# A two-layer graph attention kernel: column maxima by halves, and the second layer's first chunk prepared inside the first layer

## The chip, the cores and the metric

The kernel runs on one core of a Trainium2 chip. The metric is the device time of one execution in microseconds (us); shorter is better. The engines are called PE (TensorE, matrix products), DVE (VectorE), ACT (ScalarE), POOL (GpSimd) and SP (SyncE, which here only issues DMA transfers). [...]

## What is computed

```python
def gat_layer(x, W, adj):                  # twice, W of 512 x 1024
    Wh, Ws = split(x @ W, 2, axis=-1)
    a = softmax(Wh @ Ws.T, axis=-1) * adj   # 3327 x 3327
    return leaky_relu(a @ Wh + x, 0.01)
h = layernorm(x + gat_layer(gat_layer(x, W0, adj), W1, adj))
ba, bw = maximum(sign(h), 0), sign(weight)
return layernorm(h + relu(adj @ (ba @ bw.T)))
```

x is 3327 x 512, adj is 3327 x 3327 with about one per cent of ones, everything in float32.

## The kernel before, in words

The 3327 rows make 26 tiles of 128 (P), 13 pairs of tiles (NQ), and 7 chunks of 512 columns (NC); a half is 256 columns (HW), the output rows of one pair. A float32 product of two-by-two blocks is done with seven instead of eight block products (Strassen and Winograd's form, `seven`, L168). Its operands need sums of blocks (`left_sums` L203, `right_sums` L210), and its seven products share three PSUM banks, called X, Y and Z, which copies (L145, L183, L196 or L597, L632) and adds (L186, or L607, L622, L628) empty.

`project` (L297) makes, for one layer, the values x @ Wh-part and, with the product of the two weight halves (`product_m`, L281, named m and msum), the queries for the scores. It works from x transposed, one chunk at a time. Later chunks are loaded in a form whose 32 x 32 blocks are already in place (`load_laid`) and are turned by DVE (L338). The first chunk is loaded in rows and turned by 16 PE transposes (L326 in layer 1, L332 in layer 2) with copies out of PSUM (L333). `keys` (L371) makes the key sums and stores the blocks for the scores (`xs_d`) from POOL's queue. The queries are stored as `gs_d` and loaded again by chunk as `gs` (a tile with two buffers, shared with the weight sums `wsum`).

`attention` (L549) computes the transposed scores and then the values. Its loop (L985 to L1024) goes over v from -34 to 168. In step v it does the block products of the values for `steps[v]`, where step 13 g + q is half g and key pair q, and the scores for `ahead[v + 30]`, so the scores run 30 steps ahead; near the end of a layer only values are left. A step takes about 6 us while both are in it, and 3 us or somewhat more with one of them. In each step the work is a list of pairs (position, function); it is sorted by position, and that order is the order of the instructions on each engine. So a position sets only an order, not a time. The work of a step is:

- from the scores: the bank's adds and copies, then the running maximum over key pairs (`maximum`, L639 to L650). The first key pair of a half copies (L648), the others take a maximum (L650);
- `shift` of the pair three steps ahead at 0.0 (DVE, L736, subtracts the column maximum) and its exponential at 0.12 (ACT, L739);
- for the pair two steps ahead, `running` at 0.01 (the sum for the softmax; DVE, a copy L745 for q = 0 and an add L747 otherwise) and `masked` at 0.4 (DVE, L752, times adj), followed by block sums on POOL (L790 to L793);
- in some steps the same sums for adj in 8 bits (`halved_sums` at 0.6, `halved` at 0.61, `exact` at 0.62; L755 to L781);
- `values` (PE, L817), and at the last key pair `take_out` (L827 to L851), with which DVE empties the accumulators. It is called at positions (i + 1.4) / 7 for i = 1, 3, 5, 6, that is 0.343, 0.629, 0.914 and 1.057;
- one function of `finish` (L853 to L934) at 0.7: the reciprocal sum (`norm`: POOL's sum of totals L856, PE's pz L865), the residuals (L881, L884), and in the last layer sign, PE transposes (L905) and the binary linear product;
- entries of a dictionary `early`. In layer 1 these are the loads, turns (L253, L260) and products (L289) of layer 2's weights in the last 15 to 30 steps.

`column_max` (L666 to L709) comes when a chunk's scores are complete. It puts three functions for both halves of the chunk into the next step: the fold of two row blocks (-0.04), the maximum across partitions (0.36: turns, reductions, and small copies between groups of 32 partitions, L697 among them), and the turn back into the tile `off` (0.9, L704). The first `shift` of the chunk stands in the step after the next.

`finale` (L1114) first makes layernorm constants (`constants`: the root on ACT L1125, then DVE L1126, L1127), then the sums for the last tile pair's binary product (`product_sums`, L1192, whose instructions show as L211 to L214), and then aggregates adj @ xw (PE, L1109).

Of the kernel before, what the change touches and what calls it, by code (L numbers as in the profile page):

```python
# [9 lines left out]
F32 = mybir.dt.float32  # L10
# [20 lines left out]
def kernel(  # L31
# [193 lines left out]
    ch_lane, acc_lane, tr_lane = (ps_ch, "ch"), (ps_acc, "acc"), (ps_tr, "tr")  # L225
    w_rows, w_laid, wT, m_of, wsum_of = {}, {}, {}, {}, {}

# [6 lines left out]
    def transpose_w(l, h, k, lane):  # L234
        pool, tag = lane
        pt = pool.tile([P, D], F32, tag=tag, name=f"pwT_{l}_{h}_{k}")
        for d in range(KD):
            nc.tensor.transpose(pt[:, ts(d, P)], w_rows[l, h, d][:, ts(k, P)], ident)
        wT[l, h, k] = slot([P, D], F32, f"wTs_{l}_{h}_{k}")
        copy_out(1 if h == 0 else k, wT[l, h, k], pt)  # L240

# [55 lines left out]
    def project(l, pre):  # L297
# [18 lines left out]
        def transpose_first(lane):  # L316

            pool, tag = lane
            xTs[0] = pre.tile([P, KD, CW], F32, tag="xT", bufs=2, name=f"xT_{l}_0")
            pts = [pool.tile([P, CW], F32, tag=tag, name=f"pxt_{l}_{k}") for k in range(KD)]  # L320
            xts = [t.rearrange("r (p k) -> r k p", k=KD) for t in rows_of[0]]
            if l == 0:

                for a in range(CT):
                    for k in range(KD):
                        nc.tensor.transpose(pts[k][:, ts(a, P)], xts[a][:, k], ident)  # L326
                for k in range(KD):
                    copy_out(k, xTs[0][:, k], pts[k])
                return
            for k in range(KD):  # L330
                for a in range(CT):
                    nc.tensor.transpose(pts[k][:, ts(a, P)], xts[a][:, k], ident)  # L332
                nc.scalar.copy(xTs[0][:, k], pts[k])  # L333

        def transpose_x(c, a):
            if a == 0:
                xTs[c] = pre.tile([P, KD, CW], F32, tag="xT", bufs=2, name=f"xT_{l}_{c}")
            nc.vector.transpose(  # L338
                xTs[c][:, :, ts(a, P)].rearrange("p k (r v) -> p r k v", v=B),
                rows_of[c][a].rearrange("p r (u k) -> p r k u", u=B),  # L340
            )


        load_x(0)
        wa = pre.tile([P, KD, D], F32, tag="wa", bufs=1, name=f"wa_{l}")
# [6 lines left out]
        load_x(1)  # L352
        transpose_first(acc_lane)
        parts = sums_w(l) if l == 0 else []
# [16 lines left out]
        def keys(c, a, between=lambda: None):  # L371

            q = c * CT // 2 + a
            xT = xTs[c]
            j1, j2 = ts(2 * a, P), ts(2 * a + 1, P)
            s12 = slot([P, 2, 2, P], F32, f"s12_{l}_{q}")
            s34 = slot([P, 2, 2, P], F32, f"s34_{l}_{q}")
            of = {
                A11: xT[:, 0:2, j1], A12: xT[:, 2:4, j1], A21: xT[:, 0:2, j2],
                A22: xT[:, 2:4, j2], S1: s12[:, 0], S2: s12[:, 1], S3: s34[:, 0],  # L380
                S4: s34[:, 1],
            }
            left_sums(
                *(of[i] for i in (A11, A12, A21, A22, S1, S2, S3, S4)), between=between
            )
            to = xs_d[l][q]
            for raw in (A11, A12, A21, A22):
                nc.gpsimd.dma_start(out=to[:, raw], in_=of[raw])
            nc.gpsimd.dma_start(out=to[:, S1 : S2 + 1], in_=s12)
            nc.gpsimd.dma_start(out=to[:, S3 : S4 + 1], in_=s34)  # L390
            return of
# [157 lines left out]
    def attention(l, att):  # L549
# [5 lines left out]
        sc, top, total, off, adj, acc, gs, xs, ch = ({} for _ in range(9))  # L555
        asum, ws, out_ = {}, {}, {}
        WS = 3
# [27 lines left out]
        def scores(c, q, s):  # L585
# [53 lines left out]
            def maximum(i):  # L639
                t = sc[i, q]  # L640
                if q == NQ - 1 and pad:
                    nc.vector.tensor_scalar(
                        t[:, 1], t[:, 1], there[:, 0:1], there[:, 1:2], ALU.mult, ALU.add
                    )
                if q == 0:
                    top[i] = att.tile([P, 2, HW], F32, tag=f"top{i % 2}", bufs=1,
                                      name=f"top_{l}_{i}")
                    nc.vector.tensor_copy(top[i], t)  # L648
                else:
                    nc.vector.tensor_tensor(top[i], top[i], t, ALU.max)  # L650

            if s == 1:

                after.append((-0.05, lambda: maximum(mine[0])))
                if q == NQ - 1:
                    after.extend(column_max(c))
            if len(mine) == 1:
# [7 lines left out]

        def column_max(c):  # L666

            mine = halves_of(c)
            n = len(mine) * HW // B


            part = small.tile([P, CW // B], F32, tag="mxq", bufs=1, name=f"mxq_{l}_{c}")
            quad = small.tile([P, P // B, CW // B], F32, tag="mx4", bufs=1,
                              name=f"mx4_{l}_{c}")
            whole = small.tile([P, CW // B], F32, tag="mx", bufs=1, name=f"mx_{l}_{c}")

            def fold():
                for g in mine:
                    nc.vector.tensor_tensor(
                        top[g][:, 0], top[g][:, 0], top[g][:, 1], ALU.max  # L680
                    )

            def across():
                w = HW // B
                for i, g in enumerate(mine):
                    nc.vector.transpose(top[g][:, 1], top[g][:, 0])
                    nc.vector.reduce_max(
                        part[:, ts(i, w)],
                        top[g][:, 1].rearrange("p (r u) -> p r u", u=B), axis=AX.X,
                    )  # L690
                for a in range(P // B):
                    nc.vector.tensor_copy(quad[:B, a, :n], part[ts(a, B), :n])
                nc.vector.reduce_max(
                    whole[:B, :n], quad[:B, :, :n].rearrange("p a r -> p r a"), axis=AX.X
                )
                for a in range(1, P // B):
                    nc.vector.tensor_copy(whole[ts(a, B), :n], whole[:B, :n])  # L697

            def back():
                w = HW // B  # L700
                for i, g in enumerate(mine):
                    off[g] = att.tile([P, 1, HW], F32, tag=f"off{i}", bufs=1,
                                      name=f"off_{l}_{g}")
                    nc.vector.transpose(  # L704
                        off[g][:, 0].rearrange("p (r u) -> p r u", u=B),
                        whole[:, ts(i, w)].unsqueeze(2).to_broadcast([P, w, B]),
                    )

            return [(-0.04, fold), (0.36, across), (0.9, back)]  # L709

# [26 lines left out]

        def exponential(g, q):
            nc.scalar.activation(sc[g, q], sc[g, q], AF.Exp)  # L739

        def running(g, q):

            if q == 0:
                total[g] = att.tile([P, 2, HW], F32, tag="total", name=f"total_{l}_{g}")
                nc.vector.tensor_copy(total[g], sc[g, q])  # L745
            else:
                nc.vector.tensor_tensor(total[g], total[g], sc[g, q], ALU.add)  # L747
# [53 lines left out]
        def values(g, q):  # L801
# [21 lines left out]
            if q == NQ - 1:  # L823
                got += [((i + 1.4) / 7, lambda i=i: take_out(g, i)) for i in (1, 3, 5, 6)]
            return got
# [27 lines left out]
        def finish(g):  # L853
# [72 lines left out]
            if not last:  # L926
# [3 lines left out]
            return [  # L930
                norm, lambda: residual(0), lambda: (sign(0), fetch(1)), *free,
                lambda: turn(0), lambda: linear(0), lambda: residual(1), lambda: sign(1), *free,
# [3 lines left out]
        if last:  # L936

            early, wts = {}, {}

# [7 lines left out]
        else:  # L947

            end = len(ahead) - LOOK
            early, parts = {}, []  # L950
            for i in range(2 * KD):
# [11 lines left out]
            early[end + 3] = [(0.9, lambda: load_w(l + 1, 0))]  # L963
            n = len(steps) - end - 2
            early[end + 2] = [(0.2, begin_m)]
            for i, do in enumerate(product_m(l + 1, ch_lane)):
                early.setdefault(end + 2 + i * n // (KD * KD), []).append(
                    (0.3 + 0.4 * (i % 2), do)
                )
            early.setdefault(end + 7, []).append((0.6, lambda: parts.extend(sums_w(l + 1))))  # L970
            for i in range(4):
                early.setdefault(end + 7 + i, []).append((0.65, lambda: parts.pop(0)()))
# [141 lines left out]
    def finale(att):  # L1114
# [69 lines left out]
        def check():  # L1184
# [4 lines left out]
            nc.vector.tensor_copy(flag_i, flag)  # L1189

        constants()
        product_sums(NQ - 1)  # L1192
        load_h(0)
# [142 lines left out]
```

## Time and profile before

| what | value |
|---|---|
| time, median of 3 runs | 2627.36 us (2627.24 to 2629.74) |
| the profiled execution's own time | 2626.88 us |
| its span, first to last instruction | 2625.1 us (1.78 us lie outside) |
| granted PE clock, mean | 0.998 of full speed |
| DMA | 639 MB, 243 GB/s over the span |
| ACT L739, exponential of 128x512 | x338, 631 ns each |
| DVE L650, maximum of 128x512 | x312, 726 ns each |
| DVE L736 / L747 / L752 | x338 / x312 / x338, 735 / 745 / 705 ns each |

The profile is one execution. A row of the timeline gives start and duration in us, the engine, the line, the operation, output <- inputs, the shape and a count; brackets hold the idle time before it and the instruction whose end released it ("issue" where the profile names none). PEld is the loading of weights, which overlaps the matmuls. An engine's row of waits gives what it waited for, the total, how often, and the longest. POOL's durations are rough. The line numbers are those of the kernel before.

### The profile page before, as it was taken

How to read it: one execution, taken by the hardware profiler on the slowest of the kernel's cores; microseconds unless marked ns; L12 is line 12 of the kernel's file. 1: busy time of each engine (PE TensorE's matmuls, PEld its weight loads, DVE VectorE, ACT ScalarE, POOL GpSimd, SP SyncE). 2: the span in 40 equal slices, each digit the busy share in tenths (PEclk: the TensorE clock that was granted, in tenths of full speed). 3: DMA queues.
4: the chain of work that ended last, by engine and by line, in shares of the span. 5: the costliest groups of instructions: out<-in, count | busy, mean ns of one | idle time of the engine just before them, and what ended most of it. 6: DMA issues, size and time to landing. Idle time of an engine off the chain costs nothing. (4 is left out here: it accounts for less than half of the span.)

```text
span 2625.1 us, 40169 instructions
## 1 busy us (share of the span) xinstructions
PE 2582.4 (98%) x12552; PEld 2238.6 (85%) x12552; DVE 2116.0 (81%) x4376; ACT 785.9 (30%) x1954; POOL 1104.1 (42%) x2025
## 2 busy tenths in 40 slices
PE   9999999999999999999999999999999999999998
PEld 6888888888888888887888888888888888888787
DVE  6764888899898896777875689989899898767876
ACT  2323332333333332211332333333333333222143
POOL 3640344444444444546562144444444444455510
PEclk9999999999999999999999999999999999999999
DMA  6855777787777776787875668777787776688775
GB/s 209 296 193 180 240 242 269 232 276 249 263 245 246 267 241 223 236 254 245 284 243 179 226 223 283 250 242 265 238 283 245 236 271 233 226 263 264 260 249 171
DMA packets 308055, 639.16 MB, mean 243 GB/s; under 512 B 34855, under 2 KB 175745, under 8 KB 306298
## 3 DMA queue, kind: packets, MB, share of 16 engines
q1 hardware_dynamic: 272140, 530.29, 61.7%
q0 software_dynamic: 35664, 106.18, 11.0%
q8 instruction: 103, 1.69, 0.3%
q14 instruction: 118, 0.97, 0.1%
q10 hardware_dynamic: 30, 0.03, 0.0%
HBM read 529.69 MB, written 106.67 MB: 242 GB/s over the span
## 5 line engine op out<-in xcount | busy, mean ns | idle before, releaser
L580 PE MATMUL pZ<-gs,xs 128*128 128x256 f32 x2496 | 636.8, 379 | 2.0 <-ACT u L597 1.7
L790 POOL TENSOR_TENSOR as<-s 128x128 f32<-128x128 f32 x338 | 163.8, 485 | 1042.9 <-DVE s L752 888.2
L580 PEld LDWEIGHTS pZ<-gs,xs 128*128 128x128 f32 x2496 | 473.2, 190 | 69.2 <-ACT u L597 3.6
L817 PE MATMUL acc<-ws,s 128*128 128x256 f32 x1352 | 402.2, 379 | 0.0
L817 PE MATMUL acc<-wh,s 128*128 128x256 f32 x1352 | 355.7, 379 | 0.6 <-DVE s L752 0.4
L817 PE MATMUL acc<-ws,as 128*128 128x256 f32 x1352 | 348.0, 380 | 7.0 <-issue 4.0
L739 ACT ACTIVATE s<-s 128x512 f32<-128x512 f32 x338 | 213.4, 631 | 428.4 <-DVE s L736 428.3
L580 PE MATMUL pY<-gs,xs 128*128 128x256 f32 x1248 | 320.6, 379 | 1.7 <-ACT p L597 1.7
L817 PEld LDWEIGHTS acc<-ws,as 128*128 128x128 f32 x1352 | 255.9, 190 | 48.8 <-issue 8.9
L817 PEld LDWEIGHTS acc<-wh,s 128*128 128x128 f32 x1352 | 256.7, 190 | 36.2 <-DVE s L752 1.4
L817 PEld LDWEIGHTS acc<-ws,s 128*128 128x128 f32 x1352 | 256.0, 190 | 34.5
L650 DVE TENSOR_TENSOR top<-top,s 128x512 f32<-128x512 f32 x312 | 222.5, 726 | 73.1 <-ACT s L637 53.3
L580 PEld LDWEIGHTS pY<-gs,xs 128*128 128x128 f32 x1248 | 236.8, 190 | 35.0 <-ACT p L597 2.8
L736 DVE TENSOR_TENSOR s<-s,off 128x512 f32<-128x512 f32 x338 | 248.4, 735 | 0.1
L752 DVE TENSOR_TENSOR s<-s,adj 128x512 f32<-128x512 f32 x338 | 238.3, 705 | 8.9
L747 DVE TENSOR_TENSOR total<-total,s 128x512 f32<-128x512 f32 x312 | 232.5, 745 | 0.0
L792 POOL TENSOR_TENSOR as<-s 128x128 f32<-128x128 f32 x338 | 208.6, 617 | 26.5
L597 ACT COPY u<-pZ 128x256 f32<-128x256 f32 x312 | 115.7, 371 | 323.2 <-PE pZ L580 322.6
L817 PE MATMUL acc<-wh,as 128*128 128x256 f32 x676 | 202.5, 381 | 0.0
L791 POOL TENSOR_TENSOR s<-s 128x128 f32<-128x128 f32 x338 | 186.7, 552 | 27.4
L793 POOL TENSOR_TENSOR as<-s,as 128x128 f32<-128x128 f32 x338 | 181.8, 538 | 26.5
L622 DVE TENSOR_TENSOR s<-p,u 128x256 f32<-128x256 f32 x156 | 67.6, 433 | 139.0 <-ACT u L597 137.9
(218 smaller groups left out, 3864.0 us busy)
## 6 DMA issues: line engine op xcount, KB each, us to landing
ws<-ws_d SPq DMA_DIRECT2D x338, 512.0 KB, 3.8
xs<-xs_d SPq DMA_DIRECT2D x182, 512.0 KB, 5.9
adj<-in_adjT_dram SPq DMA_DIRECT2D x324, 256.0 KB, 4.3
xs<-xs_d SPq DMA_DIRECT2D x156, 384.0 KB, 6.4
gs_d<-gsp POOLq DMA_DIRECT2D x88, 256.0 KB, 3.0
gs<-gs_d SPq DMA_DIRECT2D x12, 1792.0 KB, 11.5
adj_d<-ab POOLq DMA_DIRECT2D x169, 112.0 KB, 3.9
ahl<-adj_d SPq DMA_DIRECT2D x78, 224.0 KB, 4.9
```

Source lines behind the costliest of these rows:

```text
L580: nc.tensor.matmul(ch[bank], xs[c, q, a][:, k], gs[c][:, b, k], start=(start and k == 0), stop=(k == 1), skip_group_check=True,)
L597: nc.scalar.copy(ch[name], ch[bank])
L650: nc.vector.tensor_tensor(top[i], top[i], t, ALU.max)
L736: nc.vector.tensor_tensor(s, s, off[g].to_broadcast([P, 2, HW]), ALU.subtract)
L739: nc.scalar.activation(sc[g, q], sc[g, q], AF.Exp)
L747: nc.vector.tensor_tensor(total[g], total[g], sc[g, q], ALU.add)
L752: nc.vector.tensor_tensor(s, s, adj[g, q], ALU.mult)
L790: nc.gpsimd.tensor_tensor(s3, a11, a21, ALU.subtract)
L791: nc.gpsimd.tensor_tensor(a21, a21, a22, ALU.add)
L792: nc.gpsimd.tensor_tensor(s2, a21, a11, ALU.subtract)
L793: nc.gpsimd.tensor_tensor(s4, a12, s2, ALU.subtract)
L817: nc.tensor.matmul(acc[g][i // 2][:, i % 2], a[i], b[i], start=(q == 0 and i % 2 == 0), stop=(q == NQ - 1), skip_group_check=True,)
```

## The change

1. The column maximum is made half by half. For the even half of a chunk all four pieces (fold, turn, across, back) stay in the step after the last score; the odd half's fold and turn go a step later, its `across` another, its `back` another.
2. At the first key pair nothing is copied: `top` comes from a maximum of the first two pairs' scores, and `total` from a second exponential of the first pair.
3. `take_out` stands at 0.34, 0.59, 0.91 and 1.06.
4. Layer 2's first chunk of x is loaded in laid form (16 transfers on SP, steps 160 to 163 of layer 1's attention), turned by DVE in steps 165 and 166, and its key sums are made in step 167. Its tile takes a buffer of `gs`. `project` of layer 2 then neither loads nor turns it.
5. `product_m` begins one step later, spread over 14 instead of 15 steps.
6. In the last layer the finish of half 11 (`g == NQ - 2`) gets an empty slot before `norm`, so all of it comes a step later.
7. `finale` calls `product_sums` before `constants`.
8. `transpose_w` copies with ACT only (layer 1's weights at the start; two of the eight copies were on DVE).

```diff
+    def turn_x(xT, a, xt):
+        nc.vector.transpose(
+            xT[:, :, ts(a, P)].rearrange("p k (r v) -> p r k v", v=B),
+            xt.rearrange("p r (u k) -> p r k u", u=B),
+        )
+    def key_sums(l, q, a, xT, between=lambda: None):
...
+        left_sums(
+            *(of[i] for i in (A11, A12, A21, A22, S1, S2, S3, S4)), between=between
+        )
+        return of
...
-        copy_out(1 if h == 0 else k, wT[l, h, k], pt)
+        nc.scalar.copy(wT[l, h, k], pt)
...
-        load_x(0)
+        if l == 0:
+            load_x(0)
+        else:
+            xTs[0] = x_first[l]
...
-        transpose_first(acc_lane)
+        if l == 0:
+            transpose_first(acc_lane)
...
-                if q == 0:
+                if q == 1:
...
-                    nc.vector.tensor_copy(top[i], t)
-                else:
+                    nc.vector.tensor_tensor(top[i], sc[i, 0], t, ALU.max)
+                elif q > 1:
                     nc.vector.tensor_tensor(top[i], top[i], t, ALU.max)
...
-                    after.extend(column_max(c))
+                    after.extend(column_max(mine[0]))
+                    for i in mine[1:]:
+                        for n, (_, do) in zip((2, 2, 3, 4), column_max(i)):
+                            early.setdefault(v + n, []).append((0.68, do))
...
-            return [(-0.04, fold), (0.36, across), (0.9, back)]
+            return [(-0.04, fold), (0.2, turn), (0.5, across), (0.7, back)]
...
         def exponential(g, q):
-            nc.scalar.activation(sc[g, q], sc[g, q], AF.Exp)
-
-        def running(g, q):
-
             if q == 0:
                 total[g] = att.tile([P, 2, HW], F32, tag="total", name=f"total_{l}_{g}")
-                nc.vector.tensor_copy(total[g], sc[g, q])
-            else:
+                nc.scalar.activation(total[g], sc[g, q], AF.Exp)
+            nc.scalar.activation(sc[g, q], sc[g, q], AF.Exp)
+
+        def running(g, q):
+
+            if q > 0:
                 nc.vector.tensor_tensor(total[g], total[g], sc[g, q], ALU.add)
...
-                got += [((i + 1.4) / 7, lambda i=i: take_out(g, i)) for i in (1, 3, 5, 6)]
+                got += [
+                    (at, lambda i=i: take_out(g, i))
+                    for i, at in ((1, 0.34), (3, 0.59), (5, 0.91), (6, 1.06))
+                ]
...
-                norm, lambda: residual(0), lambda: (sign(0), fetch(1)), *free,
+                *(free if g == NQ - 2 else []), norm, lambda: residual(0), lambda: (sign(0), fetch(1)), *free,
...
-            n = len(steps) - end - 2
+            n = len(steps) - end - 3
...
-                early.setdefault(end + 2 + i * n // (KD * KD), []).append(
+                early.setdefault(end + 3 + i * n // (KD * KD), []).append(
...
+            laid, n = [], len(steps)
+            for a in range(CT):
+                early.setdefault(n - 9 + a, []).append((0.9, lambda a=a: load_first(a)))
+                early.setdefault(n - 4 + a // 2, []).append((0.45, lambda a=a: turn_first(a)))
+            for a in range(CT // 2):
+                early.setdefault(n - 2, []).append((0.6 + a / 10, lambda a=a: keys_of_first(a)))
...
+        product_sums(NQ - 1)
         constants()
-        product_sums(NQ - 1)
```

`load_first(a)` calls `load_laid` on SP for 128 rows of the first layer's output, `turn_first(a)` calls `turn_x`, and `keys_of_first(a)` calls `key_sums`.

More of the change, by code (lines that the diff above doesn't have):

```diff
@@ L225 @@
     ch_lane, acc_lane, tr_lane = (ps_ch, "ch"), (ps_acc, "acc"), (ps_tr, "tr")
-    w_rows, w_laid, wT, m_of, wsum_of = {}, {}, {}, {}, {}
+    w_rows, w_laid, wT, m_of, wsum_of, x_first, keys_first = ({} for _ in range(7))
+    def turn_x(xT, a, xt):
[4 more added lines that the diff above has]
+    def key_sums(l, q, a, xT, between=lambda: None):
+        j1, j2 = ts(2 * a, P), ts(2 * a + 1, P)
+        s12 = slot([P, 2, 2, P], F32, f"s12_{l}_{q}")
+        s34 = slot([P, 2, 2, P], F32, f"s34_{l}_{q}")
+        of = {
+            A11: xT[:, 0:2, j1], A12: xT[:, 2:4, j1], A21: xT[:, 0:2, j2],
+            A22: xT[:, 2:4, j2], S1: s12[:, 0], S2: s12[:, 1], S3: s34[:, 0],
+            S4: s34[:, 1], "s12": s12, "s34": s34,
+        }
+        left_sums(
+            *(of[i] for i in (A11, A12, A21, A22, S1, S2, S3, S4)), between=between
+        )
+        return of
     def load_w(l, h):
@@ L321, in transpose_first @@
             xts = [t.rearrange("r (p k) -> r k p", k=KD) for t in rows_of[0]]
[L322 to L326, printed above, removed]
+            for a in range(CT):
                 for k in range(KD):
-                    copy_out(k, xTs[0][:, k], pts[k])
-                return
+                    nc.tensor.transpose(pts[k][:, ts(a, P)], xts[a][:, k], ident)
             for k in range(KD):
-                for a in range(CT):
-                    nc.tensor.transpose(pts[k][:, ts(a, P)], xts[a][:, k], ident)
-                nc.scalar.copy(xTs[0][:, k], pts[k])
+                copy_out(k, xTs[0][:, k], pts[k])
         def transpose_x(c, a):
@@ L337, in transpose_x @@
                 xTs[c] = pre.tile([P, KD, CW], F32, tag="xT", bufs=2, name=f"xT_{l}_{c}")
[L338 to L341, printed above, removed]
-        load_x(0)
+            turn_x(xTs[c], a, rows_of[c][a])
+        if l == 0:
+            load_x(0)
+        else:
+            xTs[0] = x_first[l]
         wa = pre.tile([P, KD, D], F32, tag="wa", bufs=1, name=f"wa_{l}")
@@ L373, in keys @@
             q = c * CT // 2 + a
[L374 to L385, printed above, removed]
+            of = keys_first.pop((l, q), None) or key_sums(l, q, a, xTs[c], between)
             to = xs_d[l][q]
@@ L388, in keys @@
                 nc.gpsimd.dma_start(out=to[:, raw], in_=of[raw])
-            nc.gpsimd.dma_start(out=to[:, S1 : S2 + 1], in_=s12)
-            nc.gpsimd.dma_start(out=to[:, S3 : S4 + 1], in_=s34)
+            nc.gpsimd.dma_start(out=to[:, S1 : S2 + 1], in_=of["s12"])
+            nc.gpsimd.dma_start(out=to[:, S3 : S4 + 1], in_=of["s34"])
             return of
@@ L555, in attention @@
         sc, top, total, off, adj, acc, gs, xs, ch = ({} for _ in range(9))
-        asum, ws, out_ = {}, {}, {}
+        asum, ws, out_, early = {}, {}, {}, {}
         WS = 3
@@ L664, in scores, with column_max, turn @@
             ]
[L666 to L675, printed above, removed]
-            def fold():
[L678 to L681, printed above, removed]
-            def across():
[L684 to L690, printed above, removed]
+        def column_max(g):
+            w = HW // B
+            part = small.tile([P, w], F32, tag="mxq", bufs=1, name=f"mxq_{l}_{g}")
+            quad = small.tile([P, P // B, w], F32, tag="mx4", bufs=1, name=f"mx4_{l}_{g}")
+            whole = small.tile([P, w], F32, tag="mx", bufs=1, name=f"mx_{l}_{g}")
+            t = top[g]
+            def fold():
+                nc.vector.tensor_tensor(t[:, 0], t[:, 0], t[:, 1], ALU.max)
+            def turn():
+                nc.vector.transpose(t[:, 1], t[:, 0])
+                nc.vector.reduce_max(
+                    part, t[:, 1].rearrange("p (r u) -> p r u", u=B), axis=AX.X
+                )
+            def across():
@@ L691, in across @@
                 for a in range(P // B):
-                    nc.vector.tensor_copy(quad[:B, a, :n], part[ts(a, B), :n])
+                    nc.vector.tensor_copy(quad[:B, a], part[ts(a, B)])
                 nc.vector.reduce_max(
-                    whole[:B, :n], quad[:B, :, :n].rearrange("p a r -> p r a"), axis=AX.X
+                    whole[:B], quad[:B].rearrange("p a r -> p r a"), axis=AX.X
                 )
                 for a in range(1, P // B):
-                    nc.vector.tensor_copy(whole[ts(a, B), :n], whole[:B, :n])
+                    nc.vector.tensor_copy(whole[ts(a, B)], whole[:B])
@@ L699, in back @@
             def back():
[L700 to L707, printed above, removed]
-            return [(-0.04, fold), (0.36, across), (0.9, back)]
+                off[g] = att.tile([P, 1, HW], F32, tag=f"off{g % 2}", bufs=1,
+                                  name=f"off_{l}_{g}")
@@ L711, in load_adj @@
+                nc.vector.transpose(
+                    off[g][:, 0].rearrange("p (r u) -> p r u", u=B),
+                    whole.unsqueeze(2).to_broadcast([P, w, B]),
+                )
+            return [(-0.04, fold), (0.2, turn), (0.5, across), (0.7, back)]
         def load_adj(g, q):
@@ L738, in exponential @@
         def exponential(g, q):
+            if q == 0:
+                total[g] = att.tile([P, 2, HW], F32, tag="total", name=f"total_{l}_{g}")
+                nc.scalar.activation(total[g], sc[g, q], AF.Exp)
             nc.scalar.activation(sc[g, q], sc[g, q], AF.Exp)
         def running(g, q):
-            if q == 0:
-                total[g] = att.tile([P, 2, HW], F32, tag="total", name=f"total_{l}_{g}")
-                nc.vector.tensor_copy(total[g], sc[g, q])
-            else:
+            if q > 0:
                 nc.vector.tensor_tensor(total[g], total[g], sc[g, q], ALU.add)
@@ L936, in attention @@
         if last:
-            early, wts = {}, {}
+            wts = {}
             def load_weight(k):
@@ L949, in attention @@
             end = len(ahead) - LOOK
-            early, parts = {}, []
+            parts = []
             for i in range(2 * KD):
@@ L970, in attention, with turn_first, load_first, keys_of_first @@
             early.setdefault(end + 7, []).append((0.6, lambda: parts.extend(sums_w(l + 1))))
+            def turn_first(a):
+                if a == 0:
+                    x_first[l + 1] = ops.tile([P, KD, CW], F32, tag="gs", name=f"xT_{l + 1}_0")
+                turn_x(x_first[l + 1], a, laid.pop(0))
+            def load_first(a):
+                laid.append(slot([P, P // B, P], F32, f"xr_{l + 1}_{a}"))
+                load_laid(nc.sync, laid[-1], x1_d[ts(a, P), :], P)
+            def keys_of_first(a):
+                keys_first[l + 1, a] = key_sums(l + 1, a, a, x_first[l + 1])
+            laid, n = [], len(steps)
+            for a in range(CT):
+                early.setdefault(n - 9 + a, []).append((0.9, lambda a=a: load_first(a)))
+                early.setdefault(n - 4 + a // 2, []).append((0.45, lambda a=a: turn_first(a)))
+            for a in range(CT // 2):
+                early.setdefault(n - 2, []).append((0.6 + a / 10, lambda a=a: keys_of_first(a)))
             for i in range(4):
```

## The prediction

> **What bounds the kernel now.** I read the engines' busy times first, then the list of what TensorE (PE) waited for, then the timeline at each wait.
>
> ```profile
> PE 2582.4 (98%) x12552; PEld 2238.6 (85%) x12552; DVE 2116.0 (81%) x4376; ACT 785.9 (30%) x1954; POOL 1104.1 (42%) x2025
> ```
>
> PE sets the time, and the change takes only 16 small transposes from it. What can be won is what PE does not do: 2625.1 - 2582.4 = 42.7 us idle. Some 27.2 us of it lie between matmuls, and each wait has a name (releaser: total us, times, longest):
>
> ```profile
> PE acc L817 <- issue: 4.0, 3, 1.7
> ...
> PE pX L580 <- DVE s L628: 3.5, 4, 1.2
> ...
> PE pz L865 <- POOL adj L716: 2.7, 1, 2.7
> PE pZ_wh L401 <- DVE s L205: 2.5, 1, 2.5
> PE pm L289 <- DVE wTs L260: 2.0, 1, 2.0
> PE agg L1109 <- DVE wh L212: 1.8, 1, 1.8
> ...
> PE pwT L238 <- DVE wTs L147: 1.2, 1, 1.2
> ```
>
> Apart from pz, whose releaser is POOL, all end at a DVE instruction that stood behind others in its queue. So every item below is a question of order, and of what DVE's queue holds there. A matmul record has a pace of 0.2165 us, and "lost" means start to start less that pace; it is a little more than the idle gap, which is my lower end.
>
> **Column maxima, part 1.** Timeline (start, duration, engine, line, operation), chunk 0 of layer 1:
>
> ```profile
> 270.77 0.76 DVE L704 STREAM_TRANSPOSE off<-mx 128x256 f32<-128x256 f32 x2
> 271.46 0.65 DVE L736 TENSOR_TENSOR s<-s,off 128x512 f32<-128x512 f32 x1
> 272.03 0.41 DVE L622 TENSOR_TENSOR s<-p,u 128x256 f32<-128x256 f32 x1
> 272.36 0.42 DVE L628 TENSOR_TENSOR s<-pY,u 128x256 f32<-128x256 f32 x1
> 272.83 1.13 PE L580 MATMUL pX<-gs,xs 128*128 128x256 f32 x4 [0.79 <-DVE s L628]
> ```
>
> L628 releases a PSUM bank and is late, since one step took 4.8 us of maximum work: two folds of 0.42, two turns and reductions of 0.86, seven tiny copies and a reduction (about 1.4), two L704 of 0.42. After, that step holds one half's 3.1 us; the other half's work (1.28, 1.4, 0.42) falls into the next three. The small operations that a chunk's halves shared are now done twice: +1.4 us of DVE in each of the 12 chunks with two halves, spread. The waits of this kind: gaps 0.79+1.20+0.71+0.79 = 3.5, lost 5.4. I take 4.4. If the 3.1 us are still too much, 0.
>
> **Top and total copies, part 2.** Out: 26 L648 of 0.475 (12 us) and 26 L745 of 0.547 (14 us) of DVE, little of it at a PE gap, so I book no gain. In: 26 more Exp on ACT at 0.631 = 16.4 us. ACT is 30% busy, but copies that free PSUM (u, p, c21) stand behind it. Below: no loss (DVE's subtraction comes earlier by what is removed; the masking of L752 and the sum of L747 come one step, 3 to 6 us, after their Exp, so they see nothing). Above: 0.63 at each of 26 half starts = 16.4. After an odd half's first Exp ACT idles 1.5 to 2.7 us, which hides it; after an even half's first Exp copies follow at once (424.71: Exp, then casts and copies to 426.4). Such starts with scores beside them number ten (halves 0 to 8 of both layers), which brings the ceiling to 6.3; I take 1.0, near the lower end, as only copies on the way to a full bank can count.
>
> **Take-outs, part 3.**
>
> ```profile
> 598.90 0.69 DVE L650 TENSOR_TENSOR top<-top,s 128x512 f32<-128x512 f32 x1
> 599.50 0.42 DVE L843 TENSOR_TENSOR ou<-acc,op 128x256 f32<-128x256 f32 x1
> 599.96 0.42 DVE L844 TENSOR_TENSOR ou<-acc,ou 128x256 f32<-128x256 f32 x1
> 600.48 1.10 PE L817 MATMUL acc<-ws,as 128*128 128x256 f32 x4 [1.56 <-issue]
> ```
>
> "Issue" hides the cause: PE starts right after L844 has read the bank. Position 0.59 instead of 0.629 puts L843 and L844 ahead of the adjacency sums (0.6 to 0.62), about 2 us of DVE. Three such places: gaps 1.56+1.70+0.72 = 4.0, lost 4.7; I take 4.3. Next late there are the sums, which are for a store and wanted steps later.
>
> **Layer 2's first chunk, parts 4 and 5.** At the boundary PE spends 1.93 us on 16 transposes (1243.40 to 1245.33), ACT 2.05 on four copies, then PE waits for the key sums, which stand behind DVE's last residuals (L881, L884):
>
> ```profile
> 1231.10:1240.80 9.70, 9.70 (x42) 7.79 (x41) 0.04 (x1) 0.37 (x1) 3.72 (x8) 1.00 0.85 255
> ...
> 1251.00:1252.00 1.00, 0.58 (x2) 0.57 (x3) 1.00 (x4) 0.00 (x0) 1.00 (x3) 0.84 0.99 304
> 1252.00:1253.00 1.00, 1.00 (x3) 0.55 (x3) 0.97 (x4) 0.00 (x0) 1.00 (x2) 0.50 0.89 296
> ```
>
> (Columns: window, length, busy PE, PEld, DVE, ACT, POOL, then PE's clock.) The moved work, four turns at 1.096 (L338) and eight sums at 0.42, is 7.8 us, and DVE idles 9.69 us in just those steps (first row): hidden. Were that cover gone, L841 to L851 and the residuals would be up to 7.8 us late. Two rules of the Trainium skill speak here. "VectorE: DVE Perf Modes", Rules for kernel authors, gives 128x128 transposes to TensorE if PSUM will do. By row and rule taken alone the swap is 4.38 us of DVE for 1.93 of PE, a loss of 2.5; but the 1.93 is on the path and the 4.38 is not, so I book +1.93. "TensorE: Matmul & The Clock Gate", Part 1, says that the clock is halved after an idle window of some 3.4 us. Here the idle was 2.46 us, and yet the clock stood at 0.50 from 1251.7 to 1255.1, so that eight records took 3.30 us, not 1.73. By the rule this 1.57 is not tied to the gap and stays; by the row it goes with it. I go by the row. Sum: 1.93+2.46+1.57+0.19 (the next wait, on L147) = 6.15; by the rule 4.6. I take 6.0.
> The key sums' stores stay on POOL where they were. The loads: 16 issues of about 0.49 (L128: 22 in 10.76 us) on SP in four steps, 2 us a step, where SP issues 0.75 us per 3.88 us step: hidden; the four row loads go. The new tile takes one of the two gs buffers, so the load of gs for chunk 0 waits on SP for the chunk's last query product, and SP's later loads queue behind it. It was issued at 1283.88, waits for stores of the same chunk anyhow, and was first needed at 1407.72: 0, and over 100 us of cover. The product of the weights starts one step later and ends in the same step: its transposes (0.88, L260) are then done before PE asks. Gap 2.01; I take 1.9.
>
> **The rest.** Part 6: pz waits for a sum of the totals that POOL makes only at 2433.7, behind its own queue; one step later it is ready. Gap 2.69 (+0.35 before it), but DVE, which idled only 1.52 for it, is the next late; I take 2.2. All later steps of that half's finish, its fetches, PE transposes and stores too, come a step (3 us) later; the list still ends within the last half's 13 steps, so 0, and at worst one DMA landing (4.9 us for ahl) at the end. Part 7: before wh's L212, DVE stood for
>
> ```profile
> 2496.69 1.28 ACT L1125 ACT_TABLE_LOAD   x1
> 2497.99 0.32 ACT L1125 ACTIVATE rstd<-mv,eps 128x26 f32<-128x26 f32 x1
> ```
>
> With L211 to L214 first, their inputs (ready at 2496.7) no longer wait: gap 1.84, I take 1.8; the first normalised row is later by about 1 us, which is not PE's. Part 8: two copies of 0.68 on DVE become 0.59 on ACT; the first stood 0.43 in DVE's queue (transposes done 17.43, copy from 17.86) while PE waited 1.16, which so shrinks by about 0.4.
> Not touched: waits on DMA (1.2, 1.2, 0.45, 1.1, 0.7) and the last steps of layer 2 (4.4 lost at 2456 to 2471, DVE at 14.9 of 15.5).
>
> **Sum:** 4.4-1.0+4.3+6.0+1.9+2.2+1.8+0.4 = 20.0 us. The profiled run took 2626.88 (span 2625.1 and 1.78 around it), so it would be 2606.9; the median is 0.48 above it: 2607.4.
>
> **Rivals.**
> (a) Next-late: DVE is 81% busy, so the smaller pieces and the second Exp make new waits at the PSUM adds. Then the maxima bring 0, ACT costs 5, take-outs 2.5: 2.5+6.0+1.9+2.2+1.8+0.4-5 = 9.8, time 2617.6. For it: layer 1's queue had no idle around these steps. Against: their work falls by 26 us in all.
> (b) Slower: the second Exp stalls PE at every half start. From 20+1.0 = 21 us over 26, 0.81 us each, it eats the gain. At twice its length, 1.26 each (once in the scores' copies, once in the masks), 32.8 us: 21.0-32.8, slower by 11.8, 2639. The trace speaks against both halves: masks lie a step away, and odd halves have idle ACT.
> (c) The change doesn't do what it says: waits have other releasers than I read, and only the 1.93 of transposes and 2.5 of the gap stay: 2623.
>
> **Chances:** forecast 0.76, (a) 0.15, (c) 0.05, (b) 0.04 (slower by more than 0.2% from 1.01 us a half start). The forecast's own range is from lost times in full (23.6) with 3 us for DVE's lighter load, 2601, to gaps only with ACT at 4, 2613; with part of (a), 2601 to 2616. About 0.2% (5.3 us) is what a measurement can tell from none. Faster 0.91, same 0.05, slower 0.04.
>
> **What would show it.** Right: in PE's waits no pX behind L628, no issue waits of 1.5 at the layer-1 half ends, pz, pm, agg below 0.5, no pxt in layer 2, the clock at 1.00 around the boundary, DVE busy from 1231 on. Wrong: waits of the same total under other names (pZ or pY behind ACT's u, p after a first Exp), or DVE full after 1240 so that pZ_wh waits again.

## The result and the profile after

The changed kernel takes 2614.3 us (median of 6 runs, 2612.44 to 2617.41) against 2627.3 us before (median of 6): ratio 0.9952, 95% interval 0.9942 to 0.9962. That is 10 to 15 us faster. The forecast was 20.0 us faster, 2607.4; the measured time lies inside its range, at the upper end, and 7 us of the forecast gain are missing. The profiled execution took 2613.73 us, with a span of 2611.9.

The page's busy times after the change:

```profile
PE 2578.8 (99%) x12511; PEld 2234.7 (86%) x12536; DVE 2109.5 (81%) x4422; ACT 799.8 (31%) x1978; POOL 1091.7 (42%) x2025
```

PE is busy 3.6 us less, of which 1.93 are the transposes and the rest mostly the half clock that is gone. The gaps between its matmuls fell from 27.2 to 19.2 us. What PE waited for (releaser: total us, times, longest):

```profile
PE pY L586 <- ACT p L603: 6.0, 4, 2.2
PE acc L820 <- POOL as L795: 4.1, 6, 1.2
PE pxt L347 <- DMA xr<-in_x_dram: 3.7, 1, 3.7
PE pZ L586 <- ACT u L603: 2.8, 5, 0.6
PE pz L871 <- POOL adj L719: 0.9, 1, 0.9
PE pX L586 <- ACT s L638: 0.9, 1, 0.9
PE pwT L260 <- ACT wTs L262: 0.7, 1, 0.7
```

Most of the waits that the change aimed at are gone: no pX behind DVE's add, no "issue" at the take-outs, no pm, no agg, no pZ_wh behind the key sums. The pz of 2.7 us is gone too (the 0.9 is at another place, 1193 us), and pwT fell from 1.2 to 0.7. But one that stood in before's list with 1.7 us, pY behind ACT's copy p, is now 6.0.

If the two traces are laid over each other matmul by matmul, the gain does not climb evenly. It is 1.1 us at the start of layer 1's attention and -0.5 at 919 us, after gains of 1.4 to 1.9 at single places and losses of 1.4 to 2.4 at others. It then rises to 7.2 at the layer boundary and ends at 11.6. So layer 1's attention, to which most of the forecast's 8.7 us for maxima and take-outs belonged, gave nothing. Its losses stand at the ends of two chunks: the gain falls from 1.4 to -0.1 us between 420 and 460 us (chunk 1) and from 1.3 to -2.3 between 735 and 790 us (chunk 3).

The 1.1 us at the start may be chance. The eleven kernels here that have the changed start reach the first product of the scores at 184.6 to 187.6 us in their traces; the changed kernel does so at 184.7, the kernel before at 185.8.

One of the losses in the changed kernel's timeline, at the end of chunk 1 (rows of PEld and other engines left out):

```profile
423.19 0.93 SPq L577 DMA_DIRECT2D xs<-xs_d  x2
...
425.27 0.56 POOL L778 DMA_DIRECT2D adj_d<-ab  x1
...
431.19 0.40 ACT L761 CAST ab<-adj 128x256 fp8e4<-128x256 f32 x1 [2.59 <-DMA adj_d<-ab]
...
431.70 0.36 ACT L603 COPY p<-pY 128x256 f32<-128x256 f32 x1
...
432.11 0.92 PE L586 MATMUL pY<-gs,xs 128*128 128x256 f32 x3 [1.47 <-ACT p L603]
```

PE waits for the copy p; the copy stands on ACT behind a cast into ab, the 8-bit adjacency blocks; the cast waits 2.59 us until a store of ab has landed. That tile has two buffers (L767; L764 before), and POOL stores each one a step after its cast, behind the block sums of that step. Here the store left at 425.27. The transfer's own row for this store says that it landed 5.9 us later, at 431.17:

```profile
DMA to landing us min/median/max: 5.9/5.9/5.9
```

In the kernel before, the same store (the 19th of ab) left 4.0 us after the load of xs, not 2.1, and its row says 2.7 us. It landed at 431.27, just before its cast came up:

```profile
424.55 0.93 SPq L571 DMA_DIRECT2D xs<-xs_d  x2
...
428.57 0.56 POOL L775 DMA_DIRECT2D adj_d<-ab  x1
...
431.34 0.41 ACT L758 CAST ab<-adj 128x256 fp8e4<-128x256 f32 x1
```

So the changed kernel issued this store 3.3 us earlier, but closer behind the load, and it landed only 0.1 us earlier: the wait took back 1.7 of the 2.7 us gained until then. At the end of chunk 3 it is the same: the store left 1.5 us after the load and took 6.3 us, before 3.5 and 3.4.

DVE's waits, which the prediction never opened, show the same from the other side, over the whole kernel. Before (first row) DVE already stood still for this landing 14 times, 17.3 us in all; after (second row), 20 times and 28.6 us:

```profile
DVE ab L772 <- DMA adj_d<-ab: 17.3, 14, 4.2
```

```profile
DVE ab L775 <- DMA adj_d<-ab: 28.6, 20, 3.8
```

### The profile page after: what moved, and what is told of

Same layout as the page of the kernel before. It is cut to its first block, busy times and chain, and to the rows that moved or that the text cites. A ratio compares the mean times of both kernels' runs of the same rounds, so it can differ in the third digit from the quotient of the medians.

```text
span 2611.9 us, 40070 instructions
## 1 busy us (share of the span) xinstructions
PE 2578.8 (99%) x12511; PEld 2234.7 (86%) x12536; DVE 2109.5 (81%) x4422; ACT 799.8 (31%) x1978; POOL 1091.7 (42%) x2025
## 5 line engine op out<-in xcount | busy, mean ns | idle before, releaser
L793 POOL TENSOR_TENSOR as<-s 128x128 f32<-128x128 f32 x338 | 162.7, 481 | 1052.6 <-DVE s L755 873.2
L656 DVE TENSOR_TENSOR top<-top,s 128x512 f32<-128x512 f32 x286 | 199.9, 713 | 72.9 <-ACT s L643 52.6
L795 POOL TENSOR_TENSOR as<-s 128x128 f32<-128x128 f32 x338 | 202.1, 598 | 26.5
L628 DVE TENSOR_TENSOR s<-p,u 128x256 f32<-128x256 f32 x156 | 66.5, 427 | 137.6 <-ACT u L603 136.9
```

The costliest lines, as they stand in the source:

```text
L793: nc.gpsimd.tensor_tensor(s3, a11, a21, ALU.subtract)
L795: nc.gpsimd.tensor_tensor(s2, a21, a11, ALU.subtract)
```

## The experiments

Theory A: the missing gain went into waits for ab. Theory B: the second exponential makes ACT late. Theory C: DVE's queue is the limit and finds a next late thing whatever is freed. All ratios are to the kernel before, run beside them; "worth" is a difference of two ratios times 2627 us, and has an uncertainty of 3 to 5 us.

| kernel | median us | ratio (95% interval) |
|---|---|---|
| changed | 2614.3 | 0.9952 (0.9942 to 0.9962) |
| 1 changed, third buffer for ab | 2605.7 | 0.9919 (0.9906 to 0.9932) |
| 2 changed, DVE copy for the second exponential | 2618.8 | 0.9973 (0.9963 to 0.9983) |
| 3 changed, old maxima | 2608.0 | 0.9930 (0.9917 to 0.9943) |
| 4 changed, first chunk turned by PE | 2622.2 | 0.9982 (0.9974 to 0.9989) |
| 5 old maxima and third buffer | 2604.8 | 0.9909 (0.9894 to 0.9925) |
| 6 before, third buffer | 2621.7 | 0.9975 (0.9966 to 0.9984) |
| 7 changed, store of ab early | 2604.7 | 0.9910 (0.9896 to 0.9923) |
| 8 changed, no empty slot | 2617.3 | 0.9960 (0.9946 to 0.9973) |
| 9 as 7, old take-outs | 2609.8 | 0.9928 (0.9915 to 0.9941) |
| 10 as 7, DVE copy | 2609.7 | 0.9933 (0.9921 to 0.9945) |
| 11 as 7, more pieces and slots | 2609.7 | 0.9930 (0.9917 to 0.9943) |
| 12 before, store of ab early | 2621.8 | 0.9978 (0.9970 to 0.9986) |

**1. A third buffer for ab in layer 1.**

```diff
-                [P, 7, P], F8, tag="adj_b", bufs=2, name=f"ab_{l}_{g}_{q}"
+                [P, 7, P], F8, tag="adj_b", bufs=2 if l else 3, name=f"ab_{l}_{g}_{q}"
```

> The changed kernel with a third buffer for the 8-bit adjacency blocks (ab) in layer 1's attention; nothing else differs. Theory A (the missing 7 us of the forecast went into waits for ab: with two buffers a cast on ACT and a sum on DVE wait until the store two casts before has landed, and at the chunk ends that store now leaves POOL 1 to 2 us after a load of xs and lands 5.9 to 7.9 us later): the four waits of pY behind ACT's p (6.0 us in all) fall below 1 us in layer 1, the time falls by 5 to 7 us to about 2608. Theory B (the second exponential makes ACT late): ab is only the next thing in the queue, the waits stay within 1 us, time 2613 to 2615. Theory C (DVE's maxima and sums are the limit whatever comes free): half of it, 2611.

It came out 8.7 us faster than the changed kernel, more than theory A asked for. PE's waits for pY behind p are gone from the list, and DVE's for ab are small:

```profile
DVE ab L775 <- DMA adj_d<-ab: 4.3, 6, 1.0
```

Matmul by matmul against the changed kernel, the gains stand where the casts had waited: 1.7 at 432, 1.7 at 456 to 461, 1.7 at 752, 2.5 at 780. The landing of the store after 425 is still 5.7 us; nobody waits for it now. A holds for this kernel, B and C do not.

**2. The copy into total back on DVE** (`exponential` and `running` as before).

> The changed kernel with the copy of the first exponential into total on DVE, as before, in place of the second exponential on ACT. Theory B: the second exponential costs what the forecast misses, so 4 to 7 us faster than the changed kernel, about 2609. Theory A: no part in it; ACT gains 16.4 us and DVE loses 14.2 us of work away from the path, so 2612 to 2617, rather slower than faster; the waits of pY behind ACT's p stay at 4 to 7 us.

It is 4.5 us slower by the medians, 5.5 by the ratios. B is out: the second exponential does not cost, it gains. This was outside A's own range too (2612 to 2617).

**3. The old maxima** (`column_max` for a chunk, at -0.04, 0.36, 0.9).

> The changed kernel with the column maxima made for both halves of a chunk in one step, as before. If the maxima by halves brought the 4.4 us of the forecast: 2618 to 2619. Theory A: they brought only about 1 us net in layer 1, since the wait on the adds was replaced by the wait on ab at the same chunk end; so 2613 to 2617, the pX waits behind the add come back (3.5 us) and the pY waits behind p fall from 6.0 to about 2 us.

None of the theories expected this: 6 us faster than the changed kernel. The pX waits behind the add came back as expected (3.0 us, four times) and pY behind p fell to 1.4, but the second outweighed the first by far. In its trace the store of chunk 1's end leaves 3.7 us after the load of xs and lands in 3.9 us, much as before. With two buffers for ab, part 1 of the change is a loss.

**4. Layer 2's first chunk turned by PE again** (row loads, 16 transposes, key sums in `project`; the moved loads, turns and sums left out of layer 1).

> The changed kernel with layer 2's first chunk loaded in rows and turned by PE at the layer's start, as before, its key sums there too. The trace of the changed kernel shows 6.1 us gained at this place (1.93 of transposes, the gap of 2.46, 1.57 of half clock and 0.2): 2620 to 2621. If the half clock is not tied to the gap, 1.6 less or more. If the moved loads and DVE work cost something in layer 1's last steps, less than 6: 2617.

7.9 us slower by the ratios; its trace loses 6.2 us at the boundary against the changed kernel. The gap (DVE's L205, 2.5) and the half clock return together (PE's clock is the third column from the end):

```profile
1250.00:1251.00 1.00, 1.00 (x3) 0.82 (x4) 0.97 (x4) 0.00 (x0) 1.00 (x3) 0.50 0.89 302
```

In the changed kernel the clock there is 1.00 and PE is never idle:

```profile
1243.00:1249.00 6.00, 6.00 (x29) 5.29 (x28) 5.86 (x8) 2.74 (x7) 5.92 (x4) 1.00 0.51 140
```

**5. Old maxima with the third buffer.**

> The changed kernel with the old column maxima and with the third buffer for ab. With two buffers the maxima by halves came out 6 us slower than the old ones; if that was only the wait for ab (theory A), then without that wait they must bring something: this kernel is 2 to 4 us slower than the one with three buffers alone (2605.7), so 2608 to 2610. If the maxima by halves are worth nothing or less in themselves (theory C: extra 1.4 us of DVE a chunk, and the second half's pieces make new waits), it is the same or faster, 2603 to 2606.

Same time as with the maxima by halves (0.9909 against 0.9919): once ab is out of the way, part 1 is worth nothing that these runs can tell. PE's wait of this kind is down to two of the four places even with the old maxima (chunk 0 of each layer):

```profile
PE pX L586 <- DVE s L634: 1.6, 2, 0.8
```

**6. The kernel before with the third buffer** (the line of experiment 1).

> The kernel before with the third buffer for ab in layer 1. Its trace shows two waits on ab (1.2 and 0.45 us, 2.4 lost with what hangs on them): 1 to 3 us faster than before, ratio about 0.9992. If the third buffer brings as much here as in the changed kernel (8 us), then ab was an old cost, and the change did not bring it up: theory A, as far as it blames the change, falls.

6.6 us, far more than the 1 to 3 that the two waits at PE had suggested, and near the 8.7 of the changed kernel. So ab was an old cost, and "the change brought it up" is at most a part of the story. Where it helped is telling: two of the four pX waits vanish, and "issue" at the take-outs is halved:

```profile
PE acc L817 <- issue: 1.9, 3, 0.9
PE agg L1109 <- DVE wh L212: 1.8, 1, 1.8
PE pZ L580 <- ACT u L597: 1.7, 2, 1.0
PE pX L580 <- DVE s L628: 1.6, 2, 0.8
```

DVE had been late at the adds and the take-outs partly because it had stood still for ab some steps earlier.

**7. The store of ab at the start of the next step.**

```diff
-                    after.append((0.5, lambda of=of: keep_blocks(*of)))
+                    after.append((-0.1, lambda of=of: keep_blocks(*of)))
```

> The changed kernel with two buffers for ab; the store of ab is put at the start of the next step (-0.1) on POOL's queue instead of behind that step's block sums (0.5). Theory A with its place (the store leaves late because POOL first waits for the masks, and so falls behind the load of xs): the store leaves some 2 to 6 us earlier, ahead of that load, the waits on ab mostly go, time 2606 to 2609. If the landing is slow wherever the store leaves: no gain, 2612 to 2615; if POOL, now waiting for the casts with the block sums queued behind, delays the values: slower, 2616 or more.

9.7 us faster than the changed kernel by the medians, 11.0 by the ratios, with no more memory: the place of the store on POOL's queue is the cause. At the same chunk end:

```profile
420.96 0.56 POOL L778 DMA_DIRECT2D adj_d<-ab  x1 [1.79 <-issue]
...
425.04 0.93 SPq L577 DMA_DIRECT2D xs<-xs_d  x2
...
429.43 0.41 ACT L761 CAST ab<-adj 128x256 fp8e4<-128x256 f32 x1
```

The store leaves ahead of the load, lands in 2.3 us, and the next cast that needs its buffer finds it free. With experiment 5 this is the fastest version here, some 24 us below before.

**8. No empty slot ahead of half 11's finish in layer 2.**

> The changed kernel without the empty slot ahead of the second last half's finish in layer 2 (part 6 undone). The forecast booked 2.2 for it. The trace of the changed kernel shows 3.6 gained at pz and 3.0 lost between 2437 and 2477: so 0 to 1 us slower than the changed kernel, 2614 to 2615. If the forecast is right and the later loss has another cause: 2616.5.

Slower by 3.0 by the medians and 2.1 by the ratios, whose intervals overlap. In its trace pz waits again (3.6 us in two, 2.7 the longest), yet the end stands only 0.2 us later than in the changed kernel's. Inconclusive between 0 and 3. The profiled run is the fastest of the five (2613.9; the others took 2616.1 to 2619.6). In it the gap of 2.7 us was not followed by a half clock, as it was in two of four traces (last section); that this makes up the difference in the other runs is possible, not shown.

**9. Early store, old take-outs** (part 3 undone on experiment 7).

> The kernel with the early store of ab (2604.7) with the take-outs at their old positions (part 3 undone). If the forecast's 4.3 us hold once ab no longer stands in the way: 2609. If a part of the old waits at the take-outs was itself DVE standing still for ab, as the kernel before with three buffers suggests (its waits of acc put down to issue fell from 4.0 to 1.9 us): 2606 to 2607.

4.7 us slower by the ratios, 5.1 by the medians, in keeping with the forecast's 4.3. Its trace loses 0.9 at 598 and 0.8 at 914, where the old waits stood, and 4.2 in all within the two attentions.

**10. Early store, DVE copy** (part 2's exponential undone on experiment 7).

> The kernel with the early store of ab, with DVE's copy of the first exponential in place of the second exponential. With ab in the way the copy on DVE cost about 4.5 us against the second exponential. If that was DVE's load in itself (26 copies of 0.55 at busy places), it stays: 2607 to 2609. If it was only another phase of the store of ab: 2604 to 2606. By the forecast (second exponential costs 1.0): 2603.7.

6.0 us slower by the ratios, 5.0 by the medians: with ab cured the second exponential gains as much as with ab in the way. So it was not another phase of the store of ab; DVE's load is what remains of the explanations named. The traces show only a part of it: from the first product of the scores on they differ by 2.2 us, of which 0.5 in each layer stands at the maxima of chunk 0, where PE's pX waits for 2.0 us in all instead of 0.9.

**11. Early store, odd maxima in five pieces over five steps, an empty slot for half 11 of layer 1.**

```diff
-                        for n, (_, do) in zip((2, 2, 3, 4), column_max(i)):
+                        for n, (_, do) in zip((2, 3, 4, 5, 6), column_max(i)):
...
-            return [(-0.04, fold), (0.2, turn), (0.5, across), (0.7, back)]
+            return [(-0.04, fold), (0.2, turn), (0.5, across), (0.5, spread), (0.7, back)]
```

> An attempt at a better version: the early store of ab; the odd half's maximum in five pieces over five steps (fold, turn, gather, spread, back) instead of four over three; and an empty slot ahead of the second last half's finish in layer 1 too. The trace with the early store shows 0.9 us at pX behind the odd half's pieces of chunk 0 (and 0.5 at the same place in layer 2), and 0.9 at pz: 1 to 2.5 us faster than with the early store alone, 2602 to 2604. If other DVE work is as late there: 2604 to 2606.

A miss: 5 us slower than experiment 7. The waits it aimed at are gone, but two new ones of 2.06 us stand in layer 2:

```profile
1823.40 0.43 DVE L709 STREAM_TRANSPOSE off<-mx 128x256 f32<-128x256 f32 x1
1823.76 0.70 DVE L889 SCALAR_TENSOR_TENSOR h<-h,rz,xres 128x512 f32<-128x512 f32 x1
...
1824.50 0.69 DVE L892 SCALAR_TENSOR_TENSOR h<-h 128x512 f32<-128x512 f32 x1
...
1825.23 0.69 DVE L896 TENSOR_TENSOR h<-h,x 128x512 f32<-128x512 f32 x1
...
1826.44 0.69 DVE L741 TENSOR_TENSOR s<-s,off 128x512 f32<-128x512 f32 x1
...
1827.16 0.63 ACT L747 ACTIVATE s<-s 128x512 f32<-128x512 f32 x1 [5.99 <-DVE s L741]
1827.69 0.35 ACT L603 COPY u<-pZ 128x256 f32<-128x256 f32 x1
...
1828.10 1.22 PE L586 MATMUL pZ<-gs,xs 128*128 128x256 f32 x2 [2.06 <-ACT u L603]
```

The last piece (L709) fell into a step that holds a residual (L889 to L896); the shift (L741) comes late, ACT's exponential (L747) waits for it, and the copy u behind the exponential frees the bank late. The trace loses 3.2 us at this place, a half clock included, and 1.5 at the other.

**12. The kernel before with the early store.**

> The kernel before with nothing changed but the place of the store of ab (-0.1 instead of 0.5). If the third buffer and the early store cure the same wait, as in the changed kernel, then as with three buffers: ratio 0.9975, 2620 to 2623. If the old maxima, which hold the masks back and leave POOL idle for 8 us at a chunk's end, make the early store matter less or more: outside that.

5.8 us, as with the third buffer. So with ab cured on both sides the change is worth 17.9 us (0.9978 to 0.9910) by the early store and 14.7 (0.9975 to 0.9919) by the third buffer, against 12.6 with ab in the way. The traces give less: from the first product of the scores on, those of experiments 12 and 7 differ by 12.9 us and those of 6 and 1 by 13.8, against 10.5 for before and the changed kernel.

One thing differs from the third buffer, with which two of the four pX waits behind DVE's add went: here all four stay.

```profile
PE pX L580 <- DVE s L628: 2.7, 4, 0.8
```

Against this trace, the maxima by halves of experiment 7 gain 3.3 us at the four places and give back 1.8 a few us later. The old maxima with the early store, which would tell what that is worth, were not run.

## Why the prediction was right or wrong

The sign, the range and most mechanisms were right; the sum of 20.0 was 7 too high. By its own terms:

- **Maxima, 4.4: wrong, 0 to 1.5 with ab cured, and -6 as delivered.** The step that failed is "L628 releases a PSUM bank and is late, since one step took 4.8 us of maximum work". At chunk 0 that was so: 1.6 us gained there, 1.4 of it given back seven us later, where the odd half's `across` (1.45 us of DVE) now delays the shift. At chunks 1 and 3 the queue was late because of ab too: the third buffer alone removes both waits (experiment 6), the early store makes them shorter (experiment 12), and with the third buffer the halves bring nothing (experiment 5). And by putting the masks back on time the halves moved the store of ab closer behind the load of xs (experiment 3). The old maxima had held the masks back, and with them POOL, which stood idle for 8.7 us there; by luck this kept the store clear of the load.
- **Second exponential, -1.0: wrong sign, +5 to +6** (experiments 2 and 10). The step that failed is "little of it at a PE gap, so I book no gain". ACT's side was read rightly, since the exponential hid; the 26 copies off DVE were worth money.
- **Take-outs, 4.3: right as far as the runs can tell, 4.7 with an uncertainty of 5** (experiment 9). In the traces, the three places gain 1.7, 1.9 and 0.9 us against before. Half of the old "issue" waits also went with the third buffer alone, so with ab cured a part of the 4.7 must stand elsewhere than at these three waits.
- **First chunk, 6.0: right, 6.2 in the traces** (7.9 by the ratios). DVE's idle 9.7 us did hide the turns, against the rule of the Trainium skill ("VectorE: DVE Perf Modes", Rules for kernel authors) that gives 128x128 transposes to TensorE; here the loads had already put the 32x32 blocks in place, and DVE turned only within them. The half clock went with the gap.
- **Weights' product, 1.9: too high, 0.7.** The pm wait is gone, but in those steps pz now waits 0.87 for POOL's sum of totals.
- **The slot before pz, 2.2: between 0 and 3.** Against before's trace 0.6 remain. Against that of experiment 8, 3.1 us are gained at once and 3.0 lost again by 2467 us, where the block sums on POOL (L795) are late; experiment 8 cannot say more.
- **wh first, 1.8: right, 2.0. Start, 0.4: not shown.** The trace has 1.1 at the first step of the scores, but the start varies by 3 us among traces of the same code.
- **"Not touched: waits on DMA": wrong.** They were touched through POOL's queue. PE's list showed 1.2 and 0.45 us for ab, and these were taken as the whole cost; DVE's list had 17.3. Cured, ab is worth 5.8 to 6.6 us before and 8.7 to 11.0 after, so 2 to 5 of the missing 7 us are what the change added here, with an uncertainty of some 5 us.

The two traces show where the rest is. At the ends of chunks 1 and 3 the changed kernel loses 5.0 us in all, and the maxima of chunk 0 gain 0.2, where the forecast had +4.4. These 9.2 us are more than the 8.4 by which the traces fall short of 20.0. The product and the slot lack another 2.8. Against this stand smaller gains, among them the second exponential, the start, and a wait of pD for a load of xs (1.2 us in before's list), which fell away by chance; in experiments 2, 7 and 11 there is one again.

Rival (a), that new waits arise at the PSUM banks, came nearest to what happened, with another mechanism than it named: a store, not DVE's load or ACT's exponential. What the prediction held against it was miscounted: DVE's work falls by 26 us of copies, but by its own count the halves add 12 times 1.4 us and the first chunk's turns 4.4. DVE's busy time fell by only 6.5 us. Rivals (b) and (c) are refuted: the second exponential gains, and the waits named are gone. That the terms add up is not shown; single parts undone give larger sums than the whole.

## What to carry to other kernels

Open the list of waits of every engine that releases the bottleneck, not only the bottleneck's own: a wait of 17 us on DVE looked like 1.7 on PE, and the rest of it was booked as "DVE is late". When work in front of a DMA issue moves, ask where that transfer now leaves among the others, and how many buffers stand between its landing and the next writer. A piece that is spread out to relieve one step must be placed by what the other steps hold; 0.43 us in a full one cost PE a wait of 2 us, twice.

## What the runs showed of the hardware

How long a store of ab (112 KB) took went with how closely it followed a load of xs. In layer 1 of the changed kernel the 14 stores that left less than 2 us after an issue of such a load landed in 4.6 to 8.3 us, the other 77 in 3.4 on average (1.9 to 6.8). In the kernel before it was 5.7 to 7.5 us for 11 stores, and 3.4 on average for the other 80.

Up to PE's last product, its clock fell to 0.50 only after gaps, for 3.41 us each time, but not after each: in the 14 traces after four of four gaps of 2.46 us, two of four of 2.69, one of three of 2.01, one of two of 2.06, not after the one of 2.20, and never after a shorter one. An idle stretch well below the 3.4 us of the Trainium skill ("TensorE: Matmul & The Clock Gate", Part 1) is thus enough, and the same gap can cost 1.7 us more in one execution than in the next.
